# Layer 0 of a four-layer recurrent model: two state space units of one half written stage by stage in turn

## The chip, the cores and the metric

The kernel runs on one core of a Trainium2 chip. A core has five engines that run in parallel, each with its own instruction stream in a fixed order: TensorE (PE: matmuls, with the weight loads shown as PEld), VectorE (DVE), ScalarE (ACT), GpSimd (POOL) and SyncE (SP, which issues DMAs here). They wait for each other through semaphores. The metric is the device time of one execution in microseconds (us); lower is better. The kernel before takes 1376.14 us, the median of 3 runs (1374.77 to 1376.48).

## What is computed

A batch of 2 sequences of 1024 tokens with 128 features goes through four layers. Each normalises its input, runs a sequence mixer and a feed-forward network on the same normalised input, and adds the product of the two. Only layer 0 matters here:

```python
x = L0_attn_u
xn = _layernorm(x, axis=-1)
s = _L0_attn_ref(xn, L0_attn_W_in, L0_attn_conv_w, ...)
g = _silu(_L0_ffn_ref(xn, L0_ffn_w1, L0_ffn_b1, ...))
x = x + s * g
```

Its mixer is a state space model of four heads of 64 channels with a state of 128. After a short causal convolution and SiLU, each chunk of tokens is handled as a masked product within the chunk plus the effect of a state that is carried from chunk to chunk:

```python
CB = jnp.einsum('bcln,bcsn->bcls', Cc, Bc)
M = CB[..., None] * decay * dtc[:, :, None, :, :]
Y_intra = jnp.einsum('bclsh,bcshp->bclhp', M, Xc)
states = jnp.einsum('bclh,bcln,bclhp->bchpn', dstate, Bc, Xc)
...
new = carry * d[:, :, None, None] + s
...
Y_inter = jnp.einsum('bclh,bcln,bchpn->bclhp', jnp.exp(cA), Cc, prev)
Y = (Y_intra + Y_inter).reshape(b, l, H, P) + D[None, None, :, None] * X
y = y * jax.nn.silu(z)
y = y * jax.lax.rsqrt(jnp.mean(y * y, axis=-1, keepdims=True) + EPS) * norm_weight
return y @ W_out.T
```

The two sequences of the batch don't depend on each other here. Within a sequence the state is carried forward. The feed-forward network of layer 0 is a mixture of 8 experts with 64 hidden units each, all of them computed for every token and weighted by gates of which all but the top two are zero; it depends on `xn` alone.

## The kernel before

The tokens form 16 tiles of 128, 8 per sequence, and groups of G = 4 tiles (512 tokens). The chunk of the state space model is one tile. A *unit* is the state space work of one group of one sequence: `unit(m, b, n)` is batch element b, half n (n = 0 or 1), 512 tokens. Half 1 continues the states of half 0 of the same sequence. Layer 0 has four units.

`layer0` (L654 to 757) normalises, then calls `front` for half 0 of both sequences at once (L693): projections `px` and `pz` by PE, the convolution on DVE and ACT, giving `xs` and `sz`. `steps` (L694) makes the step sizes. Then, for each half, `front` is called for both sequences when n = 1 (L727 to 729), and the units are written (L730 and 731). At the end comes the mixture, one group after another in the order 0, 2, 1, 3 (L734 to 757), and its last two DVE operations form `s * acc` and `x + s`.

A unit is a Python generator (`unit`, L524 to 640) that yields after each of its stages:

- four stages: `da` (POOL, L545), the matmul into `pd`, its `Exp` into `E` (ACT, L548);
- `wide` (POOL, L551), 8 matmuls into two `pe`, their `Exp` into `eA`;
- three stages of transposes `pt`, with `xdt` on DVE and `xst` on POOL for two of them and the copy `Bt` on ACT for the third;
- the products of C and B into `pcb`, masked into `cb` on DVE, then four products `E` times `cb` on POOL (L581);
- one stage per tile: the matmul into `pst` and a new `state` tile on DVE (L597 or L601). Half 0 makes four states, of which the last is carried to half 1; half 1 makes three and also reads the carried one;
- two stages, one per 128 channels: `py` (within the chunk, needs `E` and `xdt`), `y` on DVE (L616), `pi` (from the states, each of the four tiles reads one state), its product `t` on DVE (L624), two operations on `y` by POOL (L625, L626) and the square by ACT (L627);
- `pss`, the sums of squares, and the inverse square root (L299 to 301);
- `pyo`, the output projection, scaled into `s` by DVE and ACT in turn (L689, L687).

`together` (L643) takes generators and advances each by one stage in turn until all are done. Before the change each unit is given to it alone, so a whole unit is written before the next. In layer 3 (L1716, L1774) two units of two heads each, and the `stacked` projections of the next pair, are already given to it at once.

All matmul results of units and `front` go to banks of the pool `sa0`, which has 5 banks under one tag (L659); the mixture has its own 3 banks, `sf0`. In SBUF the tiles of a unit have two buffers each (`da`, `E`, `eA`, `xdt`, `xst`, `Bt`, `cb`, `y`), except `wide` (one), `t` (four) and `state` (six). `xs` and `sz` from `front` have two.

The order of instructions on each engine is not the order of the text. The tile framework makes it when the kernel is built, by playing the program through a timing model (`schedule_with_timeline_sim=True`, L1828): the place in the program text is an instruction's priority, and one that is ready in the model may go ahead of an earlier one that isn't. So the mixture, written last, is placed in gaps that units leave. On the chip this order is fixed. The same holds for layers 1 to 3, except that PE's order in the attention of layer 2 is written by hand.

Layer 1 begins when the memory of layer 0 is free: its first DVE operations come after the last `x` of layer 0, and its weights are loaded at that time.

Of the kernel before, what the change touches and what calls it, by code (L numbers as in the profile page):

```python
# [20 lines left out]
NB, SEQ = 2, 1024  # L21
# [621 lines left out]
def together(*parts):  # L643

    live = list(parts)
    while live:
        live = [p for p in live if next(p, p) is not p]
# [6 lines left out]
def layer0(K, x, xn, xT, w, e):  # L654
    nc, tc, c = K.nc, K.tc, K.c
    with ExitStack() as es:
# [34 lines left out]
        m = dict(H=4, back=False, xT=xT, wz=w["wz"], wx=w["wx"], cw=w["cw"], cb=w["cb"], dt_bias=w["dt_bias"], A_log=w["A_log"], D=w["D"], wo=wo, out=out)  # L691
        space = StateSpace(K, pa, sa, [m])
# [34 lines left out]
        for n in range(TPB // G):  # L727
            if n:
                space.front([(m, b, n) for b in range(NB)])
            for b in range(NB):  # L730
                together(space.unit(m, b, n))


        for g in LATE:  # L734
# [1048 lines left out]
def build(tc, io, packs):  # L1783
    nc = tc.nc
    with ExitStack() as ctx:
        pool = ctx.enter_context(tc.tile_pool(name="const", bufs=1))
        x = pool.tile([P, NT, P], F32, name="x")
        src = io["x"].rearrange("b (t p) d -> p (b t) d", p=P)
        for g in range(NG):
            nc.sync.dma_start(grp(x, g), src[:, g * G : (g + 1) * G, :])  # L1790
        xn = pool.tile([P, NT, P], F32, name="xn")
        xT = pool.tile([P, T], F32, name="xT")

        def load(into, n, by=nc.scalar):
            t = into.tile([P, packs[n].n], F32, name="w_" + n)
            by.dma_start(t, io[n])
            return View(t, packs[n])

        K = Kern(tc, load(pool, "c"))
        dram = ctx.enter_context(tc.tile_pool(name="lists", bufs=1, space=DRAM))  # L1800
        lists = {n: dram.tile([rows, P], F32, name=n) for n, rows in (("xs", T), ("ys", 2 * T))}
        views = {}
        with tc.tile_pool(name="const0", bufs=1) as pool0:
            w0 = load(pool0, "l0")
            e0 = load(pool0, "e0")
            layer0(K, x, xn, xT, w0, e0)
        later = ctx.enter_context(tc.tile_pool(name="const3", bufs=1))
        views["l3"] = load(later, "l3")
        pair = lists["xs"], lists["ys"]
        with tc.tile_pool(name="const2", bufs=1) as pool0:  # L1810
            views.update((n, load(pool0, n)) for n in ("l1", "l2"))
            layer1(K, x, xn, xT, views["l1"], {"rows": io["rows1"], "lists": pair, **{n: io[n] for n in ("sw1", "sw3", "sw2")}})
            layer2(K, x, xn, xT, views["l2"], {"rows": io["rows2"], "lists": pair})
        layer3(K, x, xn, xT, views["l3"], {"load": lambda pool: load(pool, "x3", nc.sync), "rows": io["rows3"], "lists": pair}, io["out"].rearrange("b (t p) d -> p (b t) d", p=P))
# [17 lines left out]
```

## Time and profile before

| What | Value |
|---|---|
| Median of the runs shown | 1376.14 us |
| The profiled execution's own time | 1375.22 us |
| Its span, first to last instruction | 1373.4 us |
| Mean granted TensorE clock | 0.888 |
| PE, PEld busy | 1135.3 us (83%), 791.2 us (58%) |
| DVE, ACT, POOL busy | 885.2 us (64%), 633.2 us (46%), 425.5 us (31%) |
| Layer 0, first `da` to last write of `x` | 51.7 to 221.2 us |
| Beginning of the units' first `pd` matmuls | 56.1, 89.0, 145.9, 183.9 us |

The profile is of one execution. Busy time of an engine counts its instructions; matmuls are pipelined and their ends are modelled, so a PE that is busy all the time need not be at its peak. The granted clock is the share of TensorE's full clock that the throttle allowed. Lines of the timeline give start, duration, engine, line of the program, operation, output and inputs, shape and count; a group of like instructions may be merged into one line. Batch element and half are not named in the trace; they follow from the order.

### The profile page before, as it was taken

The numbers are of one execution on the slowest core, as the hardware profiler recorded it, in microseconds if no ns is written. First come the engines' busy times: TensorE is split into PE (matmuls) and PEld (weight loads), VectorE is DVE, ScalarE is ACT, GpSimd is POOL, SyncE is SP. The second block draws the span as 40 slices with busy tenths as digits, with TensorE's granted clock in tenths as the row PEclk, the third lists the DMA queues.
The fourth block names the chain that finished last, engine by engine and source line by source line (L and its number), as shares of the span: only waits on it lengthen the run. The fifth ranks groups of instructions, "written<-read, shape, count | busy, mean of one in ns | idle before, by whom it ended". The sixth has DMA issues, their size and how long they took to land. (4 is left out here: it accounts for less than half of the span.)

```text
span 1373.4 us, 19316 instructions
## 1 busy us (share of the span) xinstructions
PE 1135.3 (83%) x6861; PEld 791.2 (58%) x6861; DVE 885.2 (64%) x2216; ACT 633.2 (46%) x1071; POOL 425.5 (31%) x420
## 2 busy tenths in 40 slices
PE   5599775888799748999999997579889918799985
PEld 2376454787798425544444433358678815577664
DVE  6645435775664686677777744987657469566456
ACT  7655925305422232354555676134452316355761
POOL 0342341027455250000000000044666521467743
PEclk9899895899999858799999998779999967799997
DMA  2000003015345200000000001024344530223411
GB/s 89 0 1 1 1 1 129 8 53 158 95 129 153 62 0 1 1 1 1 1 1 1 1 1 32 1 92 120 104 131 126 155 103 24 69 85 97 79 52 47
DMA packets 49040, 75.72 MB, mean 55 GB/s; under 512 B 7335, under 2 KB 36402, under 8 KB 48688
## 3 DMA queue, kind: packets, MB, share of 16 engines
q1 hardware_dynamic: 39632, 54.30, 12.8%
q0 software_dynamic: 8448, 14.98, 4.9%
q10 hardware_dynamic: 864, 5.21, 1.0%
q8 instruction: 54, 0.88, 0.3%
q14 instruction: 42, 0.34, 0.1%
HBM read 63.95 MB, written 12.85 MB: 56 GB/s over the span
## 5 line engine op out<-in xcount | busy, mean ns | idle before, releaser
L1425 DVE TENSOR_REDUCE mx<-pm 128x1 f32<-128x512 f32 (+3 forms) x304 | 181.8, 655 | 63.0 <-PE pm L287 60.1
L1469 ACT ACTIVATE pr<-psc 128x1024 f32<-128x1024 f32 x144 | 139.6, 1021 | 102.1 <-PE psc L287 69.4
L1189 POOL DMA_INDIRECT xb<-xs,dfrom x132 | 132.3, 1002 | 124.2 <-PE pxb L798 31.4
L1199 POOL DMA_INDIRECT ys<-yb,dto x132 | 136.4, 1033 | 99.5 <-DVE yb L1077 47.6
L1164 POOL TENSOR_TENSOR dhh<-dhh,w_c 128x1280 fp32r<-128x1280 f32 (+2 forms) x3 | 8.8, 2949 | 475.1 <-issue 381.3
L287 PE MATMUL pm<-kT,qT 32*128 32x128 f32 (+3 forms) x576 | 118.9, 359 | 15.1 <-DVE mx L1425 10.9
L287 PEld LDWEIGHTS pm<-kT,qT 32*128 32x128 f32 x576 | 68.2, 199 | 68.1 <-DVE mx L1425 48.6
L287 PE MATMUL p<-xbT,tw 128*128 128x256 f32 x368 | 103.0, 397 | 1.7 <-ACT sg L1070 1.3
L1070 ACT ACTIVATE sg<-p,tw 128x256 f32<-128x256 f32 x92 | 41.0, 473 | 95.4 <-PE p L287 90.6
L287 PE MATMUL pat<-pr,va 128*32 128x512 f32 x576 | 80.1, 622 | 0.2 <-ACT pr L1469 0.2
L293 PE MATMUL tp<-w_c,xn 128*128 128x128 f32 x64 | 19.4, 412 | 68.4 <-DVE xn L325 41.1
L287 PEld LDWEIGHTS p<-xbT,tw 128*128 128x128 f32 x368 | 64.1, 198 | 12.7 <-ACT sg L1070 3.6
L287 PE MATMUL psc<-qT,kT 32*128 32x512 f32 x288 | 63.8, 481 | 3.0 <-ACT pr L1469 3.0
L1071 DVE SCALAR_TENSOR_TENSOR hh<-p,tw,sg 128x256 f32<-128x256 f32 x92 | 42.6, 478 | 35.0 <-ACT sg L1070 23.5
L287 PEld LDWEIGHTS po<-tw,hh 128*128 128x128 f32 x368 | 54.3, 193 | 6.1 <-DVE hh L1071 2.4
L287 PE MATMUL po<-tw,hh 128*128 128x128 f32 x368 | 56.4, 277 | 1.6 <-DVE hh L1071 1.6
L293 PEld LDWEIGHTS tp<-w_c,xn 128*128 128x128 f32 x64 | 11.5, 187 | 76.3 <-issue 38.6
L287 PE MATMUL psc<-mT,onesR 32*128 32x512 f32 x288 | 53.8, 406 | 0.0
L282 ACT COPY xbT<-pxb 128x256 f32<-128x256 f32 (+3 forms) x38 | 15.2, 401 | 64.0 <-PE pxb L798 46.9
L287 PEld LDWEIGHTS psc<-qT,kT 32*128 32x128 f32 x288 | 30.9, 185 | 15.9 <-ACT pr L1469 13.5
L287 PE MATMUL pd<-uda,w_c 128*128 128x512 f32 x64 | 38.0, 702 | 0.6 <-ACT usz L517 0.6
L504 DVE SCALAR_TENSOR_TENSOR uxs<-uxr,w_l,uxs 128x512 f32<-128x512 f32 x48 | 34.9, 768 | 4.8 <-ACT uxr L282 4.8
(531 smaller groups left out, 2835.5 us busy)
## 6 DMA issues: line engine op xcount, KB each, us to landing
tw<-in_rows SPq DMA_DIRECT2D x23, 836.0 KB, 4.8
tw<-in_rows SPq DMA_DIRECT2D x39, 384.0 KB, 3.2
yt<-ys SPq DMA_DIRECT2D x24, 256.0 KB, 3.2
tw<-in_rows SPq DMA_DIRECT2D x47, 128.0 KB, 2.2
xb<-xs,dfrom POOLq DMA_INDIRECT x132
ys<-yb,dto POOLq DMA_INDIRECT x132
xs<-xn SPq DMA_DIRECT2D x8, 256.0 KB, 2.3
w_l<-in_l ACTq DMA_DIRECT2D x1, 1890.0 KB, 11.2
```

The source lines that it names most:

```text
L282: self.nc.scalar.copy(out, in_)
L287: self.nc.tensor.matmul(out, lhsT=lhsT, rhs=rhs, start=start, stop=stop)
L293: self.nc.tensor.transpose(pt[:, j, :], src(g * G + j), self.c["ident"])
L504: nc.vector.scalar_tensor_tensor(xs[:, k, :], xr[:, k, at : at + W], m["cw"][:, k, t : t + 1], xs[:, k, :], ALU.mult, ALU.add)
L1070: nc.scalar.activation(sg, p1[:, k - k0, :], AF.Silu, bias=t[:, 1536 + k : 1537 + k])
L1071: nc.vector.scalar_tensor_tensor(hh[:, k, :], p2[:, k - k0, :], t[:, 1540 + k : 1541 + k], sg, ALU.add, ALU.mult)
L1164: nc.gpsimd.tensor_mul(h, h.bitcast(F32), c["slot"][:, at].unsqueeze(2).to_broadcast(shape))
L1189: self.K.nc.gpsimd.indirect_dma_start(dst, None, self.xs, bass.IndirectOffsetOnAxis(self.of_token[:, n : n + 1], 0))
L1199: d = self.K.nc.gpsimd.indirect_dma_start(self.ys, bass.IndirectOffsetOnAxis(self.to[:, n : n + 1], 0), src, None, bounds_check=2 * T - 1, ...
L1425: nc.vector.tensor_reduce(mx[:, starts.index(a), g, j : j + k], tile[0][:, : k * m].rearrange("p (j m) -> p j m", m=m), AX.X, ALU.max)
L1469: K.nc.scalar.activation(pr, ps, AF.Exp, scale=scale)
```

## The change

The two units of one half are given to `together` at once, so that their stages are written in turn: the first `da`, `pd` and `Exp` of sequence 0, then those of sequence 1, then the second ones of sequence 0, and so on to the output projection. `front` of half 1 still stands between the two pairs, and the mixture still comes last.

```diff
         for n in range(TPB // G):
             if n:
                 space.front([(m, b, n) for b in range(NB)])
-            for b in range(NB):
-                together(space.unit(m, b, n))
+            together(*(space.unit(m, b, n) for b in range(NB)))
```

The instructions, their operands and the numbers of buffers stay as they are. What differs is the order of the text, and with it the priorities, the order in which tiles are asked for, and the order that the framework makes from them.

## The prediction

> **What bounds the kernel now.** I read the page's busy rows and slices first, then the stretches of layer 0, the timeline at the places where one unit hands over to the next, the waits of layer 0, and last the layer 3 timeline, where pairs are already written in turn. No engine bounds the whole (PE 83% busy, DVE 64%), so the question is what bounds the 169.5 us of layer 0 that the change touches, from the first `da` at 51.7 us to the last write of `x` at 221.2 us. I cut this time where units begin: unit (batch 0, half 0), unit (1, 0), `front` of half 1, unit (0, 1), unit (1, 1). The stretches view (length, then busy time and instructions of PE, weight loads, DVE, ACT, POOL, granted clock, DMA share, GB/s):
>
> ```profile
> 51.70:89.00 37.30, 36.48 (x180) 22.84 (x181) 13.45 (x31) 23.47 (x30) 19.66 (x18) 0.94 0.00 1
> 89.00:123.00 34.00, 34.00 (x215) 24.86 (x215) 14.88 (x34) 17.11 (x25) 16.56 (x15) 1.00 0.01 1
> 123.00:146.00 23.00, 20.80 (x78) 10.81 (x79) 16.49 (x28) 20.47 (x29) 0.00 (x0) 1.00 0.00 0
> 146.00:184.00 38.00, 26.61 (x142) 17.56 (x143) 15.07 (x30) 24.06 (x30) 17.33 (x15) 0.84 0.00 1
> 184.00:221.20 37.20, 26.35 (x159) 21.50 (x157) 11.61 (x32) 11.97 (x20) 13.97 (x12) 0.78 0.04 14
> ```
>
> PE is full in the first two stretches, because the mixture (the gated feed-forward, L734 to 757) fills what a unit leaves; its last matmul stands at 171 us. After that a unit runs alone: in the last stretch PE has 26.35 us of work in 37.2 at a clock of 0.78, and all others are under 40%. There a chain of latencies is the bound. The timeline (start, duration) at the hand-overs shows why the units don't overlap:
>
> ```profile
> 88.73 0.47 PE L287 MATMUL pyo<-wo,uy 128*128 128x128 f32 x2
> ...
> 89.03 0.59 PE L287 MATMUL pd<-uda,w_c 128*128 128x512 f32 x1
> ```
> ```profile
> 122.85 0.47 PE L287 MATMUL pyo<-wo,uy 128*128 128x128 f32 x2
> ...
> 123.15 0.59 PE L287 MATMUL px<-xT,w_l 128*128 128x512 f32 x1
> ```
> ```profile
> 183.31 0.77 PE L287 MATMUL pyo<-wo,uy 128*128 128x128 f32 x2
> ...
> 183.88 1.06 PE L287 MATMUL pd<-uda,w_c 128*128 128x512 f32 x1
> ```
>
> Each time the next unit's first bank (`pd`, or `px` of `front`) follows the first `pyo` of the unit before, its last bank, by 0.3 to 0.6 us. Likewise PE stood idle for 13.4 us before 51.69 us with `xT` complete and didn't do the `px` of half 1. I read it as: the five banks of pool `sa0` are given out in the order in which the program asks for them. A unit holds the queue until it has asked for its last bank. The waits (engine and tile, for whom: total us, times, longest) agree; POOL waits longest for `pd`, with `da` of the next unit in both of its buffers:
>
> ```profile
> POOL uda L545 <- PE pd L287: 47.9, 11, 26.0
> ACT ut L627 <- POOL uy L626: 24.8, 6, 13.0
> DVE ur L299 <- PE pss L287: 23.8, 3, 12.3
> POOL uy L625 <- DVE uy L616: 22.8, 4, 7.8
> ```
>
> **What the Trainium skill says.** "Perfetto Trace Analysis", Identifying Performance Opportunities: consistent bubbles "can mean there isn't enough SBUF/PSUM for the next tile to be allocated"; the 47.9 us above are such bubbles. "TensorE: Matmul & The Clock Gate", What's actually happening: PE's clock is halved by default and released by activity; the trace agrees, a `pd` matmul of 0.59 us in the full stretch lasts 1.06 us or more in the sparse ones. "ScalarE: Activation LUTs", What ACT_TABLE_LOAD costs: about 1283 ns per change of set; the rows of this stretch have 34 loads at 1283 ns, 43.6 us of ACT's 97.1. So the order of `Exp`, `Gelu` and `Silu` matters on ACT.
>
> **The change, part by part.** No instruction, byte or buffer is added or removed; four units are paired into two, and the bank queue goes a, b, a, b. All work behind 221.2 us (layers 1 to 3) starts once layer 0's memory is free, so what layer 0 gains moves the end one for one, if the later order stays as it is. The sum is made per pair, to the first `pyo` of its later unit:
>
> 1. `da`, `pd`, `Exp`: eight in place of four. POOL alone needs 8 x 1.04 = 8.3; unit (0,0) took 6.5 for its four `pd` (55.6 to 62.1), so 13.
> 2. `pe`, `pt`: in unit (1,0) from 97.0 to `pcb` at 101.6, 4.5, bound by PE; two, 9. `wide` (1.04 each, one buffer) and `xst` (1.05 each) run below it.
> 3. `pcb`, `cb`, first product on POOL: 101.6 to 103.7, 2.2; the second is hidden below the first's products.
> 4. The products of `E` and `cb` on POOL: 2 x 4 x 1.27 = 10.1.
> 5. From there to the first `y` addition: 7.8, 6.9, 5.7 and 2.3 in the four units. Here the six buffers of `state` come in: a pair wants eight (four each). In half 1 the third new state of unit a has to wait until both `pi` groups have read the carried one, and the second stands behind `py` of b. So no hiding: 5.7.
> 6. `y` on POOL: four of (1.13 + 1.27) = 9.6.
> 7. Square to `pyo`: 121.1 to 122.9, 1.7.
>
> Sum 51.3. Now it is 55.6 to 122.9 = 67.3 for the first pair and 145.9 to 211.0 = 65.1 for the second. A nearer row warns: in layer 3 a pair of two-head units, written in turn, takes
>
> ```profile
> 1317.40 1.02 PE L287 MATMUL pd<-uda,w_c 128*128 128x512 f32 x2
> ...
> 1362.93 2.05 PE L287 MATMUL pyo<-fwo,uy 128*128 128x128 f32 x8
> ```
>
> 45.5 us. My own steps for it give some 35 (half of 1, 4 and 6 and the rest whole: 6.5 + 9 + 2.2 + 5 + 5.7 + 4.8 + 1.7). The excess of 10 is static order: engines there wait for other work that came later than planned. I add half of it, 5, and take 56 per pair; the ends are 51 (no excess) and 67 (the ratio 45.5/35 on 51.3). First pair: -11. `front` of 23 us moves up unchanged (its DVE work is 16.5 of it). Second pair: -9. The part behind the first `pyo` (211.0 to 221.2, 10.2) has two units' `pss` and `pyo` instead of one, but at full clock (16 `pss` in 1.7 instead of 3.0): +1. Together -19; the ends are -31 and +4.
>
> Cover: the mixture must still fit below. At full clock a unit has about 18 us of PE (its rows' share of the full stretch 89 to 123), `front` 10, a mixture group 12.3 (four `ph` and `pg` pairs at 1.48, `po` 5.4, `pgt` 1.0): 4 x 18 + 10 + 4 x 12.3 = 131. From 52.7 us that is 184, plus 3.7 from the last `pss` to the last `x`: 188. That is the floor, 33 below now; at 202 the mixture fits with 14 to spare. Moved with the pair: `Sqrt` (four table loads now, at least two after), 16 scaled copies to `s`, no DMA. The ACT queue holds `Gelu` behind `Exp` of both units, and the DVE product of `hT` waits for it; PE's `po` is next.
>
> The profiled execution was 1375.22 us with a span of 1373.4 (1.8 around it); the median is 0.9 above it. 1373.4 - 19 + 1.8 + 0.9 = **1357**.
>
> **Rivals.** A measurement of this kernel can't tell under 0.2% (2.75 us) from no change.
>
> - *Lockstep as summed* (-31 to -8: 1345 to 1368), predicted 1357. For it: the hand-overs, the 47.9 us, the empty last stretch.
> - *More than that*, down to the PE floor and a calmer ACT (fewer switches between `Exp` and `Gelu`): -31 to -38, 1338 to 1345. Against it: layer 3's excess.
> - *The state buffers and banks jam.* `pst` of both units sit in two of five banks while waiting for a state, and `py` and `pi` follow one by one: four rounds of about 6 us in place of 10.1 + 5.7, +8 in each pair: -3, about 1373. Together with the full ratio of layer 3 it comes to no change, 1376. A bank turn now takes 67.3/40 = 1.7 us; only at that mean pace does the pair lose its gain.
> - *Slower: the mixture is left over.* It stands last in priority. Place: after the second pair. Price: a group alone is at least 12.3 us of PE, some 15 with its chain. If units end at 199, 1.5 groups left make it even; with 2.5 left, layer 0 ends at 199 + 37 = 236, 15 late: 1391. Against it: four groups were done in 118 us beside units; for it: a pair asks twice for PE and ACT at once, and stretches where PE is full leave nothing.
> - *The change doesn't do what it says*: if banks were not given out in program order, the planner would have overlapped the units already and nothing would move. The hand-overs speak against it.
>
> **How the numbers follow.** Lockstep 0.60, more 0.07, jam 0.15, of it 0.10 faster by over 0.2% and 0.05 within, no overlap at all 0.03 (within), mixture left over 0.15. Faster 0.60 + 0.07 + 0.10 = 0.77, same 0.08, slower 0.15. Range 1340 to 1379: it leaves out the lower half of the second case (0.04) and most of the slower one (0.13). The likeliest case alone is 1345 to 1368.
>
> **What would show it.** Right: `pd` of both batches alternate from 55 us on; the POOL wait for `pd` falls from 47.9 to under 20; the first `px` of half 1 stands near 111, the last `x` of layer 0 near 202; the clock after 184 us is above 0.78; layers 1 to 3 keep their length of 1152 us. Wrong: the `pd` phase longer than 16 us per pair, long POOL idle before the first `y` (state buffers), mixture groups after the units' end, or a later layer whose length differs by more than 5 us, since the order of those is made anew as well.

## The result

The changed kernel takes 1370.79 us, the median of 15 runs, and the kernel before 1376.12 us in the runs beside them. The ratio is 0.9954 with a 95% interval from 0.9943 to 0.9965. So it is faster: the medians differ by 5.3 us (0.39%), and the ratio puts it at 0.46%. I had forecast 1357 us, a gain of 19; the direction was right and the time lies in the range, but the gain is between a quarter and a third of the forecast. In six runs below (`p_both`, `s_both`, `p_hold`, `p_both_hold`, `p_notab`, `s_notab`) the kernel before, run beside them, took 1413.53 or 1407.66 us, so of these only layer 0 is compared with the others.

The profiled span went from 1373.4 to 1369.3 us. Layer 0 ends at 217.8 us in place of 221.2, which is 3.4; layers 1 to 3 take 1151.5 in place of 1152.2. The stretches of layer 0 of the changed kernel, cut near the same places (length, then busy time and instructions of PE, weight loads, DVE, ACT, POOL, granted clock, DMA share, GB/s):

```profile
51.50:89.00 37.50, 34.50 (x145) 20.16 (x146) 8.01 (x12) 29.52 (x36) 15.78 (x16) 0.95 0.00 1
89.00:117.50 28.50, 28.50 (x204) 21.21 (x202) 16.65 (x45) 8.88 (x13) 19.08 (x17) 1.00 0.00 1
117.50:146.00 28.50, 26.36 (x124) 16.43 (x123) 19.98 (x36) 23.79 (x35) 1.47 (x2) 1.00 0.00 1
146.00:184.00 38.00, 31.85 (x157) 22.73 (x157) 13.58 (x32) 31.00 (x39) 15.85 (x15) 0.87 0.00 0
184.00:217.80 33.80, 21.43 (x142) 18.99 (x142) 11.97 (x29) 5.68 (x11) 15.08 (x13) 0.72 0.05 15
```

The last stretch is as empty as before: PE has 21.43 us of work in 33.8, at an even lower clock (0.72 against 0.78). New is ACT with 31.00 us of 38 between 146 and 184 (24.06 before). The hand-over fits my reading of it: the first `px` of half 1 follows the first `pyo` of the pair by half a microsecond, in the timeline of the changed kernel:

```profile
117.42 0.69 PE L287 MATMUL pyo<-wo,uy 128*128 128x128 f32 x4
...
117.94 1.02 PE L287 MATMUL px<-xT,w_l 128*128 128x512 f32 x2
```

The waits of layer 0 after the change (engine and tile, for whom: total us, times, longest):

```profile
POOL uda L545 <- PE pd L287: 44.3, 10, 28.5
...
POOL uwide L551 <- PE pe L287: 22.9, 3, 14.9
...
POOL uy L625 <- DVE ut L624: 13.0, 4, 6.5
```

POOL's wait for `pd` did not go away. Its longest part, 28.5 us (26.0 before), is still `front` of half 1, during which POOL has the next two `da` done and nothing else to do. The wait for the one `wide` buffer has grown from 2.4 us in all to 22.9.

The clearest view cuts layer 0 only once, at the first `pd` matmul of half 1. First the kernel before, then the changed one:

```profile
51.70:145.90 94.20, 91.17 (x470) 58.41 (x470) 44.72 (x92) 60.95 (x83) 36.23 (x33) 0.98 0.00 1
145.90:221.20 75.30, 53.06 (x300) 39.15 (x299) 26.78 (x62) 36.13 (x49) 31.30 (x27) 0.81 0.02 7
```
```profile
51.50:146.30 94.80, 89.36 (x469) 57.80 (x469) 44.94 (x93) 62.48 (x84) 36.33 (x33) 0.98 0.00 1
146.30:217.80 71.50, 53.27 (x299) 41.72 (x299) 25.25 (x61) 36.39 (x49) 30.92 (x27) 0.80 0.02 7
```

I call these the first and the second stretch from here on. The first holds half 0 and `front` of half 1. It has 470 matmul records before and 469 after and takes 94.2 and 94.8 us. Counted by their tiles (`pgt`, `ph`, `pg`, `po`), 185 of these are the mixture's in both kernels, and 39 of the mixture's stand behind them. Nothing was gained there. The second went from 75.3 to 71.5, which is the whole gain.

### The profile page after: what moved, and what is told of

It is laid out like the page before. It is cut to its first block, busy times and chain, and to the rows that moved or that the text cites. A ratio compares the mean times of both kernels' runs of the same rounds, so it can differ in the third digit from the quotient of the medians.

```text
span 1369.3 us, 19321 instructions
## 1 busy us (share of the span) xinstructions
PE 1134.2 (83%) x6861; PEld 793.5 (58%) x6861; DVE 885.1 (65%) x2216; ACT 634.7 (46%) x1072; POOL 425.2 (31%) x420
## 5 line engine op out<-in xcount | busy, mean ns | idle before, releaser
L293 PEld LDWEIGHTS tp<-w_c,xn 128*128 128x128 f32 x64 | 11.5, 187 | 75.8 <-issue 38.7
L287 PE MATMUL pcum<-kv,w_c 128*128 128x512 f32 x64 | 35.3, 652 | 2.1 <-DVE prod L1286 1.6
L287 PE MATMUL pd<-uda,w_c 128*128 128x512 f32 x64 | 34.9, 647 | 0.9 <-ACT usz L517 0.9
```

Of the source, the lines that this page charges most:

```text
L287: self.nc.tensor.matmul(out, lhsT=lhsT, rhs=rhs, start=start, stop=stop)
L293: self.nc.tensor.transpose(pt[:, j, :], src(g * G + j), self.c["ident"])
```

## Experiments

I had two theories for the missing 15 us. Theory 1: the mixture sits between the stages in the fixed orders of PE and ACT, with its table changes. Theory 2: the pair itself is long for lack of buffers (two of `da`, one of `wide`, six of `state`, five banks). I compare the ends of layer 0 (the last write of `x`), because the later layers vary by themselves, as shown below. Two kernels that were run twice ended layer 0 at 210.9 and 211.8, and at 208.9 and 211.4; I read nothing from differences of 2.5 us or less between single runs. Names beginning with p have pairs in turn, those with s serial units.

### The mixture left out

In both kernels, L734 to 755 (after) go, and the last line of the mixture adds `s` alone:

```diff
-            pt = sf.tile([32, G, P], F32, name="pgt", tag="ps")
...
-            nc.vector.tensor_mul(grp(s, g), grp(s, g), acc)
```

> Leaves the mixture out of layer 0: x + s is written instead of x + s * silu(mixture), so the output is another one. Pairs in turn. Theory 1 (the pair's stages are long because the mixture sits between them in the fixed order of PE and ACT): the stretch from the first pd to the weights of pe falls from 19.2 us (pair of half 0) and 22.5 us (half 1) to about 13 each, a pair takes about 51 us to its pyo, and the last x of layer 0 stands near 187 us instead of 217.8. Theory 2 (two da buffers, one wide buffer, six state buffers and five banks make the pair long by themselves): the stretch stays at 18 or more, a pair takes 57 or more, and layer 0 ends after 197 us.

> Leaves the mixture out of layer 0 in the same way, units one after another as before. Both theories: a unit alone takes 27 us as in the last stretch of the kernel before, so layer 0 ends at about 52 + 4 + 27 + 27 + 23 + 27 + 27 + 10 = 197 us. Theory 1: about 10 us later than the pairs without the mixture. Theory 2: within 4 us of them, as with the mixture (3.4).

Measured: 1341.77 and 1343.13 us beside 1375.96; last `x` at 187.1 in turn and 191.6 serial. The two stretches, in turn and then serial:

```profile
51.40:117.30 65.90, 57.03 (x285) 40.46 (x286) 27.53 (x68) 24.98 (x43) 35.92 (x33) 0.82 0.00 1
117.30:187.10 69.80, 48.99 (x261) 38.18 (x259) 31.82 (x62) 29.49 (x42) 33.54 (x27) 0.76 0.03 8
```
```profile
51.40:124.30 72.90, 57.89 (x284) 37.41 (x285) 32.36 (x75) 30.67 (x49) 36.28 (x33) 0.83 0.00 1
124.30:191.60 67.30, 42.40 (x261) 31.89 (x259) 25.30 (x54) 27.48 (x39) 33.09 (x27) 0.83 0.03 8
```

Without the mixture the first stretch does gain by taking turns: 65.9 against 72.9. PE had 15 us of room in it (57.89 busy of 72.9). With the mixture PE has 3 us of room (91.17 of 94.2), and the same edit brings nothing. That is the answer for the first stretch. It also corrects a number behind the forecast: bare units of half 0 take 23 and 25 us each (52.6 to 75.5 and 76.0 to 101.4), not the 33 I saw, and the bare pair 41.8.

For the pair in turn theory 1 had its figures: the `pd` phases fell to 10.9 and 10.7 us, and the last `x` stands at 187.1. The serial control speaks against it: it ends at 191.6 and not at 197. The mixture costs about 30 us either way (217.8 - 187.1 = 30.7 and 221.2 - 191.6 = 29.6), so over the whole of layer 0 its place between the stages doesn't eat a gain that pairs would otherwise have: theory 1 in this form falls. Nor does a full PE explain all that is missing, since with room on PE taking turns is worth 4.5 us in all: 7.0 in the first stretch, less 2.5 in the second.

### Gelu replaced by Exp

```diff
-                nc.scalar.activation(hT[:, k, :], ph, AF.Gelu, bias=e["b1"][:, k : k + 1])
+                nc.scalar.activation(hT[:, k, :], ph, AF.Exp, bias=e["b1"][:, k : k + 1])
```

> The mixture's Gelu is computed as Exp (another output), so ACT needs no table change between the mixture and the units' Exp. Pairs in turn. Theory 1, ACT part: the stretch from pd to pe falls from 19.2 and 22.5 us to 15 or less, and layer 0 ends at 208 us or earlier. If the mixture hinders through PE's fixed order and not through ACT's table changes: stretch 18 or more, end within 4 us of 217.8. Theory 2: the same, unchanged.

> The same exchange of Gelu for Exp with units one after another. Theory 1, ACT part: units gain less than pairs, since a unit asks for half as many Exp at once: layer 0 ends at about 217 us instead of 221.2, so the pairs win by 9 us or more. Otherwise the difference between pairs and units stays at 3 to 4 us.

Measured: 1366.46 and 1372.79 beside 1375.96; last `x` at 217.7 and 218.3. The changed kernel's layer 0 doesn't move (217.8), the serial one by 3. Between 50 and 90 us the table loads of the changed kernel fell from 12 to 3, and the `pd` phase of half 0 still takes 17.7 us. I took this as the end of the question of tables, too early: of the 13 loads between 146 and 184 us 12 remained, since `Silu` kept alternating with `Exp`. See the last pair of runs.

### One buffer more at a time, and one half alone

To make room, one of the mixture's tiles (`gTh`, for `wide` also `acc`) has one buffer.

```diff
-            new = tile("state", [P, nx, P], 6)
+            new = tile("state", [P, nx, P], 4 + H)
...
-            da = tile("da", [P, per, H, P])
+            da = tile("da", [P, per, H, P], H - 1 if H > 2 else 2)
...
-        wide = tile("wide", [P, G, H, 64], 1)
+        wide = tile("wide", [P, G, H, 64], H // 2)
```

The three edits are those of `p_state8`, `p_da3` and `p_wide2`. `H`, the number of heads, is 4 in layer 0 and 2 in layer 3, so layer 0 gets eight `state`, three `da` and two `wide`, and layer 3 keeps its buffers.

> Pairs in turn, with eight state buffers instead of six in layer 0 (a pair needs eight); the mixture's gTh gets one buffer instead of two to make room. If the state buffers set the late part of a pair (theory 2): the time from the end of the products E times cb to the first y addition of half 1 falls from 6.5 us to 3 or less, the stretch from there to the first pyo shrinks too, and layer 0 ends 5 to 8 us before 217.8. Theory 1: that gap falls by some 3 us in half 1, half 0 is unchanged, layer 0 ends 0 to 4 us earlier.

> Pairs in turn, with three da buffers instead of two in layer 0; gTh one buffer. If the pace of pd is set by da and its buffers (theory 2): the stretch from the first pd to pe falls from 19.2 and 22.5 us to 15 or less. Theory 1 (it is set by the mixture on PE and ACT): 18 us or more in both pairs, layer 0 ends within 3 us of 217.8.

> Pairs in turn, with two wide buffers instead of one in layer 0; the mixture's gTh and acc get one buffer each. In the pair of half 0, 8.2 us lie between the pe of the first unit and the pe of the second, filled with mixture matmuls, since the planned order had the second wide copy end late. Theory 2: that gap goes (under 2 us), step pe to pcb falls from 14.7 to 9 us, layer 0 ends 3 to 6 us earlier. Theory 1: the mixture matmuls only move and are missing later, end within 2 us.

> Only the pair of half 0 is written in turn; half 1 unit by unit as before. From the spans of the two kernels: half 0 in turn gained 5.7 us to its first pyo and lost 5.4 in front behind it, half 1 gained 6.3 and lost 2.9 behind it. If the two halves act independently: layer 0 ends within 1 us of 221.2. If half 0 in turn also carries mixture work out of the way of half 1: 3 us or more off.

Measured: `p_state8` 1370.16, `p_da3` 1377.55, `p_wide2` 1361.42, `p_first` (half 0 in turn, half 1 serial) 1377.29, beside 1375.87. Last `x` at 213.2, 221.7, 210.9 and 223.5.

The state buffers do what the step said: in half 1 the gap between the last product of `E` and the first `y` addition goes from 6.5 us to nothing. But the `pd` phase before it grows from 22.5 to 28.0 (144.5 to 172.5), so 4.6 us are left. The third `da` shortens the `pd` phase of half 0 from 19.2 to 13.5 and then `pe` of unit b starts 14.8 us after `pe` of unit a has ended in half 1; no gain. The second `wide` puts the `pe` of both units side by side in both halves (before, in half 0, 8.2 us lay between their starts) and is worth 6.9 us: 4.4 in the first stretch (94.8 to 90.4), where PE is now busy for 88.8 of 90.4 us, the rest in the second. `p_first` agrees that half 0 in turn brings nothing: 223.5 against 221.2 with no half in turn.

### Both buffers, and the mixture held back

`p_both` joins `wide` and `state` (with one buffer each of `gT`, `gTh`, `acc`), `s_both` does so with serial units. `p_hold` makes the third group of the mixture wait, in PE's order only, for the first `pd` of half 1 and the fourth for the first `pcb` of half 1; `p_both_hold` has both edits.

```diff
-                K.mm(pt[:, j, :], gates4[:, g * G + j, :], c["ident"])
+                d = K.mm(pt[:, j, :], gates4[:, g * G + j, :], c["ident"])
+                q = {2: m["pd1"], 3: m["pcb1"]}.get(LATE.index(g))
+                if j == 0 and q is not None:
+                    tc.add_manual_dep(d.ins, q.ins.name, ...)
```

> The pair in turn with two `wide` buffers and eight `state` buffers (for room, `gT`, `gTh` and `acc` of the mixture have one buffer each). Alone, the second `wide` buffer brought the last `x` of layer 0 from 217.8 to 210.9 us and the two state buffers to 213.2. If the buffers are two independent terms of the pair's length, they add: last `x` at 205 to 208, `pe` of both units side by side and no gap between the last product of `E` and the first `y` addition in half 1. If the buffers only shift the wait to whatever comes next (PE, which the mixture fills), no more than the better of the two: 210 to 213.

> Control: the kernel before, units one after another, with the same buffers as the run beside it (two `wide`, eight `state`, one each of `gT`, `gTh`, `acc`). A unit alone uses one `wide` and four states at a time, so if the buffers are what the pair lacks, nothing moves here: last `x` at 220 to 222 (221.2 before). If the gain comes from the mixture with fewer buffers, or from any new order, it shows here too: last `x` at 211 to 216.

> The changed kernel with its own buffers; the third group of the mixture may not be placed ahead of the first `pd` of half 1 on PE, the fourth not ahead of the first `pcb` of half 1 (an order on PE's own queue, no wait is added on the chip). If the mixture's early place costs the first pair its gain while the last stretch stands bare (PE 21.4 of 33.8 us busy at a clock of 0.72), the first pair shortens from 61.5 to some 50 us, the second grows by less, and the last `x` stands at 208 to 213. If a group costs its 7 to 8 us wherever it stands, the last `x` stays at 216 to 220. If the last group ends behind the units, it is later than 220.

> Both buffers and the mixture's third and fourth group held as in the run before. If buffers and the mixture's place are independent terms, the last `x` is at 197 to 203 and the whole some 1350 us. If the mixture's place is no term, it is as with the buffers alone, 205 to 213; if the fourth group comes out last, later than that.

Measured: last `x` at 208.9, 224.3, 228.2 and 217.8 (1408.86, 1416.93, 1426.93 and 1417.75 beside 1413.53). With the same buffers serial units end no earlier (224.3 against 221.2), so the gain is the pair's. The control is clean for the end alone: its first stretch is 106.6 us and its second 66.1, in place of 94.2 and 75.3, so the mixture's single buffers move the order too. `p_both` lies between what two independent terms (205 to 208) and the better one alone (210 to 213) were to give. Holding the mixture back costs 9 to 10 us; with the mixture's place as the cause it was to gain 5 to 10. The stretches of `p_hold` show how:

```profile
51.50:137.00 85.50, 77.56 (x396) 53.83 (x397) 35.38 (x79) 48.84 (x68) 36.17 (x33) 0.90 0.00 1
137.00:228.20 91.20, 66.32 (x373) 47.40 (x371) 37.57 (x75) 48.98 (x64) 32.76 (x27) 0.87 0.02 6
```

Some 73 matmuls went from the first stretch to the second. The first got 9.3 us shorter than after the change (94.8), the second 19.7 longer (71.5), and PE is still idle for 24.9 us in it. The timeline of PE in `p_hold` has one place of it (in brackets the idle time before, and for whom):

```profile
169.77 0.79 PE L287 MATMUL po<-w_e,hT 128*128 128x128 f32 x2 [9.25 <-DVE hT L750]
...
176.02 1.95 PE L287 MATMUL pe<-w_c,uwide 128*128 128x128 f32 x16
```

A `po` of the held group waits 9.25 us for `hT`, and `pe` of unit b stands behind it in PE's order. The mixture put there did not fill the bare places; the pair waited behind it. Other places weren't tried.

### The bare pair with buffers, the other half alone, and times in rounds

> As the pair in turn with the mixture left out (its product with `s` too: `x` is `x` + `s`), and with two `wide` and eight `state` buffers. Without these buffers the bare pairs took 41.8 and 54.4 us from the first `pd` to the first `pyo`, and the last `x` stood at 187.1. If buffers hold the bare pair of half 1 (its gap of 7.7 us between the last product of `E` and the first `y` addition), that pair comes to 45 to 48 and the last `x` to 179 to 182. If the pair's own chain bounds it, 53 to 55 and 185 to 188.

> Half 0 unit by unit as before, half 1 in turn. From the spans of the two kernels (67.2 and 23.1 us before for half 0 and `front`, 58.8 and 13.1 for half 1 and its tail after the change) the last `x` is at 217 to 219: the whole gain lies in half 1, and half 0 in turn gives 5.7 us that `front` takes back. If the second pair is short only because the first one has let more of the mixture be done, it is at 220 to 224.

> The pair in turn with two `wide` buffers, timed. One look gave 1361.4 us beside 1375.9 and the last `x` at 210.9. If the end of layer 0 carries through, -10.3 us against the kernel before (ratio 0.9925); what one look gave would be 0.9895, of which some 3 us lie in the later layers' order, fixed for this kernel. I expect 0.988 to 0.992.

> Two `wide` and eight `state` buffers, timed. Last `x` at 208.9 in one look on a chip with a lower clock, 2 us before that of two `wide` alone. If the later layers were alike, ratio 0.991; in the one look they were some 2 us longer than the kernel before's would be. I expect 0.990 to 0.997 and, against two `wide` alone, no gain: 1362 to 1370 us where the kernel before takes 1376.

`p_nomix_both` is `p_nomix` with both buffers; `p_second` has half 0 serial and half 1 in turn:

```diff
-            together(*(space.unit(m, b, n) for b in range(NB)))
+            if n != 0:
+                together(*(space.unit(m, b, n) for b in range(NB)))
+            else:
+                for b in range(NB):
+                    together(space.unit(m, b, n))
```

`p_second`: 1365.65 us beside a median of 1376.63, last `x` at 216.7. Its two stretches are 94.4 and 70.8 us. Half 1 in turn alone has the whole gain of the change.

`p_nomix_both`: 1325.31, last `x` at 180.9, as the buffers were to give, but not where I had put it. The pair of half 1 took 56.9 us (113.8 to 170.7), not 45 to 48: the gap of 7.7 is gone, and its `pe` to `pcb` phase went from 14.9 us to 23.8 (124.3 to 148.2), with an alternation of `Silu` of the front's `xs` and `Exp` on ACT, a table load at each step. The gain lies in half 0 and in the tail.

Timed against the kernel before in 5 rounds: two `wide` 1365.32 us, ratio 0.9934 (0.9910 to 0.9958), above the 0.988 to 0.992 that I expected; both buffers 1363.75 us, ratio 0.9912 (0.9890 to 0.9935). The first interval overlaps that of the change itself (0.9943 to 0.9965), so in the time of the whole kernel the second `wide` alone is not told apart from it. The second doesn't meet it, so the pair with both buffers beats both kernels. It ends layer 0 at 211.4, no earlier than two `wide` alone (211.8). Compared with the change that is 6.4 us in layer 0; in the profiled executions its later layers are 5.0 us shorter too (1357.9 - 211.4 = 1146.5 against 1151.5), which is less than executions of one kernel differ by.

### All tables out

The timeline of ACT in the changed kernel, in the `pd` phase of half 1 (start, duration, engine, line, operation):

```profile
151.17 1.28 ACT L548 ACT_TABLE_LOAD   x1
152.46 1.09 ACT L548 ACTIVATE uE<-pd 128x512 f32<-128x512 f32 x2
153.57 1.28 ACT L505 ACT_TABLE_LOAD   x1
154.86 0.63 ACT L505 ACTIVATE uxs<-uxs 128x512 f32<-128x512 f32 x1
155.51 1.28 ACT L744 ACT_TABLE_LOAD   x1
156.80 0.69 ACT L744 ACTIVATE hT<-ph,w_e 128x512 f32<-128x512 f32 x1
157.51 1.28 ACT L505 ACT_TABLE_LOAD   x1
```

The pair's `Exp` (L548), the front's `Silu` (L505) and the mixture's `Gelu` (L744) take turns, and each brings its load. From 137.3 to 176.3 ACT is busy for 38.53 of 39.00 us, with 16 loads of 1.28. So I replaced all `Silu` and `Gelu` of layer 0 by the identity (L505, L517, L744, L754), in turn and serial:

```diff
-                nc.scalar.activation(xs[:, k, :], xs[:, k, :], AF.Silu)
+                nc.scalar.activation(xs[:, k, :], xs[:, k, :], AF.Identity if m["H"] == 4 else AF.Silu)
```

> The changed kernel with identity in place of every Silu and Gelu of layer 0 (the values change, the instructions' number and shapes don't), so that Exp's table stays loaded save for the square roots. If table loads hold the front and the pair of half 1: the `pd` stretch of half 1 falls from 22.5 us to 13 to 16, front and second pair together from 28.5 + 58.8 to some 72 to 78, the last `x` from 217.8 to 203 to 208. If the loads only fill time in which ScalarE would wait for PE anyway, the last `x` is at 214 to 218.

> Control: the same in the kernel before, units one after another. If the loads cost the pairs more than serial units (13 against 9 in the stretch from 146 to 184 us), the last `x` moves less than in the run beside it, from 221.2 to 214 to 219, and taking turns is then worth 8 to 14 us. If they cost both the same, it moves as far as in turn, and taking turns is worth some 3 to 5 us here too.

Measured: 1389.32 and 1390.04 us beside 1407.66; last `x` at 203.9 in turn and 200.3 serial. In turn, then serial:

```profile
48.00:139.80 91.80, 91.80 (x470) 60.16 (x471) 44.85 (x93) 39.25 (x66) 36.37 (x33) 0.94 0.00 1
139.80:203.90 64.10, 50.90 (x300) 39.85 (x298) 28.01 (x61) 19.13 (x34) 33.04 (x27) 0.81 0.02 8
```
```profile
47.90:138.20 90.30, 90.30 (x469) 58.61 (x469) 45.04 (x93) 41.81 (x71) 36.23 (x33) 0.98 0.00 1
138.20:200.30 62.10, 45.93 (x300) 36.08 (x299) 27.28 (x61) 20.30 (x34) 32.35 (x27) 0.88 0.03 9
```

In turn it went as the loads had it: `pd` phase of half 1 from 22.5 to 14.1 us (139.8 to 153.9), last `x` at the low end, of which 3.5 us lie ahead of the first `da` (48.0 in place of 51.5). The control went further: serial units gain more from this edit (second stretch 75.3 to 62.1, -13.2, against 71.5 to 64.1, -7.4), and taking turns isn't worth anything here (+2.0 in the second stretch, +1.5 in the first). So the idea that loads ate the pairs' gain is refuted. Both kernels get shorter without the loads, the serial one more, but not by the loads alone: in its second stretch the loads fall from 13 to 4, which is 11.5 us of the 13.2, and the granted clock is 0.88 in place of 0.81; in turn they fall from 14 to 2, 15.4 us, and only 7.4 are gained. And in the first stretch PE is now busy for all of 91.80 and all of 90.30 us: with 463 to 470 matmul records this stretch took 89.3 us or more in every run.

## Why the prediction was wrong

**What bounds the kernel.** I showed two stretches in which PE was full (36.48 of 37.30, 34.00 of 34.00) and then took 11 us off the pair that lies in them. This is the step that failed: "First pair: -11", with "`front` of 23 us moves up unchanged"; pair and `front` together came to +0.7. A pair of half 0 can only be shorter there if matmuls of the mixture move behind it, and the part called "Cover" took it as given that they would ("the mixture must still fit below"). They didn't: 469 of 470 matmul records stand in the same stretch, the mixture's 185 among them. The pair went from 66.7 to 61.5 us (122.9 - 56.1 and 117.4 - 55.9, both from the first `pd` matmul; the 67.3 of the prediction begins with its weight load) and `front` from 23.0 to 28.9, as `pss`, `pyo` and the scaling of both units, and the mixture, now lie in it; the sum of the two is the same within 0.7. That a full PE is the reason is shown by leaving the mixture out, where the same edit takes 7.0 us off this stretch, and by leaving out the loads instead, where PE is busy for all of it and the edit takes nothing off. `p_hold` did move matmuls behind it: the stretch fell to 85.5 us, and the second one rose by more.

The floor of 131 us of PE at full clock was about right as a sum (144.2 us busy before and 142.6 after, at a mean clock of 0.90), and it misled: it counts a whole whose first part is full and whose last part has a bound of its own. The page's 83% for PE over the span hid the same. The Trainium skill, "Perfetto Trace Analysis", Identifying the Most-Contended Engine, warns that matmul busy share is no good measure of how near PE is to its peak and offers the share of the peak arithmetic rate and the busy share of weight loads instead. Here the weight loads were at 58.41 of 94.20 us, and the matmul busy share, 97%, was the one that told what this edit could gain. The prediction also took POOL's wait for `pd` for the bubbles of that page, which speaks there of the engine that should be saturated; POOL was busy for 31% of the span.

**Step by step.** From the first `pd` to the first `pyo`, forecast against half 0 and half 1 of the changed kernel, in us:

| Step | Forecast | Half 0 | Half 1 |
|---|---|---|---|
| 1. `da`, `pd`, `Exp` | 13 | 19.2 | 22.5 |
| 2. `pe`, `pt` to `pcb` | 9 | 14.7 | 8.5 |
| 3. `pcb` to the first product | 2.2 | 1.9 | 2.0 |
| 4. products of `E` and `cb` | 10.1 | 9.8 | 9.9 |
| 5. to the first `y` addition | 5.7 | 3.7 | 6.5 |
| 6 and 7. `y`, square, `pyo` | 11.3 | 12.1 | 9.0 |
| excess | 5 | | |
| Sum | 56 | 61.4 | 58.4 |

Steps 3 to 7, whose rows I had measured on POOL, held as a sum (27.5 and 27.4 against 29.3). Step 1 in both halves and step 2 in half 0, on PE and ACT, were priced as if a unit had these engines to itself. In half 0 the mixture stands between them, and in half 1 ACT does, with loads: without loads step 1 is 14.1 and the pair 51.1 us (139.8 to 190.9), against my sum of 51.3 without excess. Two serial units need 52.9 there (138.2 to 191.1). So the sum for the pair was good and the figure it was set against was not: of the 65 us of serial units, 12.2 go with the loads (65.1 - 52.9), and not all 65 were a chain of latencies that a second unit could fill. There 9 loads fewer are 11.5 us; the rest, and what the higher clock gives (0.91 in place of 0.86), is not separated.

**The other terms.** Second pair -9: it was -6.7. Tail +1: it was +2.9 (13.1 us behind the first `pyo`). The clock there was not full, as I had assumed, but 0.63 (0.50 before), for 61 matmul records in place of 31. With +5.9 for `front` and -5.2 for the first pair this makes -3.1, and the first `pd` began 0.2 earlier; layer 0 ended 3.4 earlier. The direction was right through the second pair alone. The ends of my sum were off as well: 51 and 67 for each pair with +1 for the tail give -29 and +3, not -31 and +4, and the rival "down to the PE floor" ran to -38 where the floor lay at -33. Layers 1 to 3 kept their length (1151.5), as said.

**The rivals.** The state buffers jam: right as a place in half 1 (6.5 us, gone with eight buffers). That its 1373 is nearest in time is luck: it put +8 on each pair, and eight buffers gave back 4.6 us in all. `wide`, which I had called hidden below PE, was worth as much (6.9 and 6.0 us in two runs). The mixture left over did not happen: its last `Silu` is at 173.3 us. The hand-over in program order fits the changed kernel, but no run changed the number of banks, so neither it nor the banks' part in the jam is shown.

**The signs.** The `pd` of eight in a row, the length of layers 1 to 3: right. POOL's wait for `pd` under 20 (44.3), `px` near 111 (117.9), last `x` near 202, clock above 0.78 (0.72): wrong. A `pd` phase "longer than 16 us per pair" and "long POOL idle before the first `y`" were named as signs of a wrong forecast and both came (19.2 and 22.5 us; 6.5 us in half 1).

**What stays open.** Why the second stretch gains by taking turns at all: it is 3.8 us shorter with the mixture and the loads (and 4.5 in `p_second`), but 2.5 longer without the mixture and 2.0 longer without loads, and the last two are within what I read as nothing. In each case the order is made anew, and no run tells apart which part of the order gives it.

## What to carry to other kernels

Before overlapping two chains, look at the stretch in which they run, not at the span: where one engine is full there, a shorter chain only hands its time to whatever else that engine has in the same stretch (here -5.2 and +5.9). Take the length of a chain for such a sum from a run or a stretch in which it runs alone, since its length beside filler work says how long the filler is. And when two pieces are written in turn, give every tile with one buffer a second one: here a second `wide` took another 6.0 to 6.9 us off layer 0, where taking turns itself took 3.4, though in the time of the whole kernel only the pair with both buffers stood out from the change.

## What the runs showed that I had not expected

- The Trainium skill, "ScalarE: Activation LUTs", What ACT_TABLE_LOAD costs, gives about 1283 ns for a load and 2.66 us for a change of set with a drain. The trace agrees on the load, 1.28 us; the drain does not show, since the next instruction starts 0.01 us later. Not expected was that it is a matter of whole stretches: 16 loads in 39 us of a full ACT. Taking one of three functions out of the alternation removed one load of 13 there.
- Layers 1 to 3, to which no edit was made, took from 1142.6 (`p_nomix_both`) to 1155.2 us (`p_state8`) in the runs beside 1376. The traces show that an edit in layer 0 changes the order there too: the sequence of DVE instructions in these layers differs between the kernel before and the changed one. That the order makes the lengths differ is not shown. One kernel run twice, `p_wide2`, had 1148.8 and 1147.9, but the 15 executions of the changed kernel alone spread over 11.2 us (1363.45 to 1374.68).
